# Last products of a graph layer taken by halves of TensorE's rows, and its bias added by transfers, in a planned four-layer kernel

## The chip, the cores and the metric

One NeuronCore of one Trainium2 chip runs the whole program in one launch. The metric is the device time of one execution in microseconds (us). The kernel before took 2096.2 us in the median of three runs (2094.66 to 2099.83). The profile pages and the trace come from one further, profiled execution. The engines are named as in the profile: PE is TensorE's matmul, PEld its weight load, DVE is VectorE, ACT is ScalarE, POOL is GpSimd, SP is SyncE, which here only issues transfers.

## What is computed

Four graph layers follow one another on `x` of 8 batches, 2048 nodes and 64 channels, with one 2048 x 2048 adjacency `adj`. Each ends in a residual add and a layer norm. The first one is the one that the change touches:

```python
# layer 0: w[n,k] and b[n] come from each node's embedding of 16 numbers
w = einsum('nd,dkio->nkio', embedding, weight)       # weight: 16 x 3 x 64 x 64
b = einsum('nd,do->no', embedding, bias)
As = [I, A, 2 A A - I]
x_g = einsum('knm,bmc->bnkc', As, x)
x = layernorm(x + einsum('bnki,nkio->bno', x_g, w) + b)
# layer 1: attention with scores s1[i] + s2[j], leaky relu, mask, softmax, elu
# layer 2: (A + I) (x W^T + b) / row sums
# layer 3: three steps of v = W2 relu(W1 [v, A v] + b1) + b2
```

All of it is in f32. The host only lays data out: `adj` and its transpose, `weight` as 192 rows (k, i) by 1024 columns (d, o).

## The kernel before

**Tiles.** The 8 batches are held as four pairs (`p`), two batches of 64 channels side by side in 128 columns: `SX[p]` is 128 nodes x 16 tiles x 128. Nodes also fall into four chunks (`c`) of 512, four tiles each. A *sweep* (lines 1087 to 1122) multiplies one source, such as `SX[p]`, by all of the adjacency: for each chunk 16 products of 128x128 by 128x512 into one PSUM bank (`acc`, line 1106). The adjacency comes from device memory in tiles of 512 KB for every sweep, by SP's queue, through a ring of six buffers (`fetch`, line 244).

**Layer 0.** For a pair, a sweep gives y1 = A x (`y1_chunk`, line 527), stored both transposed, in device memory (`y1_cols`), and as nodes by channels (`SA`, `SB`). A second sweep gives y2 = A y1 (`y2_evict`). Then `second_pass` (line 584) takes the last products, tile by tile: x, y1 and y2 of 128 nodes, transposed, against the weights for 16 embedding dimensions. To use all of TensorE's 128 rows, x and y1 of one batch are stacked on top of each other, 64 channels each, in `xgT` (`stacks`, line 559): x by four transposes and two half copies, y1 by a transfer. One full product with `w01` (128 rows) covers both terms; y2 needs a product of 64 rows per batch with `wk2`, and the two batches' products of this kind run in the two halves of TensorE's rows. So a half of a tile, one `yp` of two PSUM banks, has two full products and one pair of halves (line 609), and the next half takes them in the opposite order. `add_terms` (line 622) scales each of 16 blocks of 64 columns by the node's embedding number (ACT, line 633; for pair 0 every second half on DVE, line 636), sums them by a tree (line 645), and adds them to `SX[p]` (line 647). `first_norm` (line 654) adds the embedding bias `eb` (line 658) and starts the layer norm. `eb` is made once from 16 products of 16 rows (`embedding_bias`, line 376).

**Layer 1.** `scores` finds row maxima on DVE (line 740). `weights` makes the attention weights: two DVE adds (lines 818 and 831) and two ACT functions (826 and 834) for each of 16 tiles, two halves and four pairs; then products with 64 columns for each batch, the two batches in the two halves of TensorE's columns (line 845).

**Layers 2 and 3** are again sweeps with small products at their ends; layer 3 of the last two pairs is one joint product by quarters (line 1219).

**What sets the order.** Nothing is ordered by the hardware alone. Each step is a Python generator; before each piece of work it yields an engine and what it waits for. `Plan` (lines 38 to 110) keeps a time for every engine, adds a cost by formula for each piece, and always emits the piece that could begin first, with ranks for ties, `SLACK` added to what TensorE waits for, and `BACK`, an offset in us for named steps. Sweeps have the last rank: they fill what is left of TensorE's time. The engines then run their own instructions in exactly this order and wait on semaphores. Row tiles of `adj` are loaded at due times of the plan (line 436), and ACT reduces each to a row sum (line 446), from which DVE makes a reciprocal (line 450). The small weights of layers 2 and 3 are centred on DVE (lines 395 to 408) and multiplied on TensorE (`ps_w`, lines 406 to 420), with a copy by ACT between (line 407). Copies that either ACT or DVE can make all go through line 368. POOL issues the transfers of masks, rows and broadcasts (s1b and mb of 1 MB, line 778; mask rows, lines 727 and 813), `sums_of_a`, which adds blocks of the adjacency in device memory by adding transfers (line 1168), and the stores.

## Time and profile before

| | us |
|---|---|
| three runs, median | 2096.2 (2094.66 to 2099.83) |
| the profiled execution | 2099.04 |
| its span, first to last instruction | 2097.3 |
| start of the first product | 6.5 after the span's start |
| start of the first and the last run of line 845 | 447.1 and 1655.8 |
| VectorE: adds of `eb` (line 658), 16 of 0.684 | 10.9 |
| half copies into `xgT` (line 368): ACT 24 of 0.578, DVE 8 of 0.688 | 13.9 and 5.5 |

How to read the profile: the page gives the busy time of each engine and its share of the span, then the same in 40 slices, in tenths. A view of waits lists who waited for whom: us in total, times, the longest. A timeline lists instructions by start, merged where they are alike: start, us from the first start to the last end, engine, line, what is written from what, TensorE's active rows and columns, shapes, and count. A product in f32 is recorded as two instructions. A matmul's end is modelled and overlaps the start of the next one, so the distance from start to start tells what one costs. Windows give each engine's busy time in a stretch, the granted clock of TensorE (1.00 is full speed), the DMA engines' busy share and GB/s.

### The profile page before, as it was taken

To read this page: it belongs to the slowest core of one execution; us is meant where nothing else is said; L and a number is where in the kernel's file an instruction comes from. 1 tells how busy PE (TensorE), PEld (TensorE's weight loads), DVE (VectorE), ACT (ScalarE), POOL (GpSimd) and SP (SyncE) were. 2 spreads that over 40 slices of the span, in tenths; PEclk is the share of its full clock that TensorE was granted. 3 is DMA by queue.
4 is the path that set the end of the run, shared out by engine and by line. 5 is a ranking of instruction groups with operands and counts; after the bars stand their busy time and mean duration, and the time that the engine had idled before them with its cause. 6 is when DMAs were issued, how large, how long until landed. Compare 5 with 4: busy or idle time off the path is not lost.

```text
span 2097.3 us, 19052 instructions
## 1 busy us (share of the span) xinstructions
PE 2065.0 (98%) x6325; PEld 917.1 (44%) x6325; DVE 1461.5 (70%) x1873; ACT 989.0 (47%) x1797; POOL 257.6 (12%) x406
## 2 busy tenths in 40 slices
PE   8999999999999999999999999998999999999997
PEld 3444444444443444444444444443443455444443
DVE  2216756998799999989987979999979732121224
ACT  0014533378877667666266676723757521000002
POOL 2210101211121111112112111001101000000000
PEclk9999999999999999999999999999999999999999
DMA  9798857865475678779969978779787678777785
GB/s 294 257 331 286 299 185 240 277 191 121 130 231 154 161 242 296 235 228 281 336 196 289 286 251 310 245 263 379 226 273 253 217 256 265 268 263 272 265 281 184
DMA packets 221157, 525.22 MB, mean 250 GB/s; under 512 B 21171, under 2 KB 29491, under 8 KB 216691
## 3 DMA queue, kind: packets, MB, share of 16 engines
q1 hardware_dynamic: 170562, 360.20, 51.0%
q0 software_dynamic: 46272, 161.70, 25.1%
q10 hardware_dynamic: 4224, 2.10, 0.4%
q8 instruction: 50, 0.82, 0.2%
q14 instruction: 49, 0.39, 0.1%
HBM read 492.28 MB, written 63.11 MB: 265 GB/s over the span
## 4 chain that ended last, share of the span: by engine, by line
PE 88%; issue 5%; DVE 4%; DMA 2%; ACT 0%; POOL 0%; POOLq 0%; ACTq 0%; DVEq 0%
PE acc L1106 44%; PE yp L609 15%; PE po L845 11%; PE acc L1219 11%; DVE junk L740 2%; PE ps_u L1041 2%; DMA a<-in_adj_t 2%; PE acc L1095 1%; PE acc L1203 1%; DVE terms L645 1%; PE pf L879 1%; PE ps_emb L991 1%; PE ps_sv L690 1%; PE ps_v L1061 0%; PE ps_xT L680 0%
## 5 line engine op out<-in xcount | busy, mean ns | idle before, releaser
L1106 PE MATMUL acc<-a,SX 128*128 128x512 f32 x1152 | 523.7, 600 | 12.5 <-DMA SX<-in_x 6.5
L1106 PE MATMUL acc<-a,SB 128*128 128x512 f32 x768 | 348.6, 597 | 0.4 <-DMA a<-in_adj_t 0.4
L1106 PEld LDWEIGHTS acc<-a,SX 128*128 128x128 f32 x1152 | 214.5, 192 | 276.9 <-issue 259.2
L826 ACT ACTIVATE e<-e,sv 128x1024 f32<-128x1024 f32 x256 | 279.6, 1149 | 80.3 <-DVE e L818 79.5
L633 ACT ACTIVATE terms<-yp,emb_sb 128x128 f32<-128x128 f32 x896 | 243.7, 390 | 130.7 <-PE yp L609 111.9
L831 DVE TENSOR_TENSOR e<-e,mb 128x2048 f32<-128x2048 f32 x128 | 290.4, 2286 | 19.9 <-ACT e L826 19.2
L818 DVE TENSOR_TENSOR e<-s1b,mk 128x2048 f32<-128x2048 f32 x128 | 289.5, 2285 | 8.6 <-PE po L845 7.9
L740 DVE CUSTOM_DVE_ANT_0 junk<-s2b,mr 128x2048 bf16<-128x2048 f32 x128 | 293.0, 2289 | 2.7
L834 ACT ACTIVATE e<-e 128x2048 f32<-128x2048 f32 x128 | 245.0, 1918 | 76.7 <-DVE e L831 76.4
L609 PE MATMUL yp<-SH,xgT 128*128 128x512 f32 x512 | 244.2, 606 | 0.0
L845 PE MATMUL po<-e,SX 128*64 128x512 f32 x1024 | 233.6, 598 | 0.0
L1106 PEld LDWEIGHTS acc<-a,SB 128*128 128x128 f32 x768 | 142.1, 191 | 170.3 <-issue 168.4
L609 PEld LDWEIGHTS yp<-SH,xgT 128*128 128x128 f32 x512 | 90.9, 189 | 137.3 <-issue 131.1
L645 DVE TENSOR_TENSOR terms<-terms 128x512 f32<-128x512 f32 (+1 forms) x176 | 130.0, 739 | 18.5 <-ACT terms L633 14.1
L813 POOL DMA_DIRECT2D mk<-by_col x128 | 71.1, 567 | 518.9 <-DVE e L818 418.3
L845 PEld LDWEIGHTS po<-e,SX 128*64 128x64 f32 x1024 | 67.9, 136 | 147.8 <-issue 135.8
L609 PE MATMUL yp<-SH,y2T 64*128 64x512 f32 x512 | 129.9, 619 | 0.8 <-DVE SB L368 0.8
L1106 PE MATMUL acc<-a,SA 128*128 128x512 f32 x256 | 117.6, 594 | 1.6 <-DMA a<-in_adj_t 1.6
L1219 PE MATMUL acc<-a,t 128*128 128x512 f32 x192 | 85.4, 592 | 0.0
L609 PEld LDWEIGHTS yp<-SH,y2T 64*128 64x128 f32 x512 | 43.2, 185 | 79.6 <-issue 73.7
L636 DVE SCALAR_TENSOR_TENSOR terms<-yp,emb_sb,terms 128x128 f32<-128x128 f32 x128 | 34.6, 344 | 54.8 <-PE yp L609 41.4
L1106 PEld LDWEIGHTS acc<-a,SA 128*128 128x128 f32 x256 | 47.1, 190 | 58.2 <-issue 54.3
(236 smaller groups left out, 1727.0 us busy)
## 6 DMA issues: line engine op xcount, KB each, us to landing
a<-in_adj_t SPq DMA_DIRECT2D x520, 512.0 KB, 5.4
mr<-by_row POOLq DMA_DIRECT2D x64, 512.0 KB, 6.4
mk<-by_col POOLq DMA_DIRECT2D x128, 256.0 KB, 5.6
an<-in_adj SPq DMA_DIRECT2D x16, 1024.0 KB, 11.3
a<-a_plus_i SPq DMA_DIRECT2D x32, 512.0 KB, 5.1
a<-sb SPq DMA_DIRECT2D x24, 512.0 KB, 4.4
a<-sc SPq DMA_DIRECT2D x24, 512.0 KB, 4.3
a<-sd SPq DMA_DIRECT2D x24, 512.0 KB, 4.5
```

The costliest lines, as they stand in the source:

```text
L609: nc.tensor.matmul(yp[:, e, :], lhsT=y2T[rows, cs] if k2 else xg[:, e, cs], rhs=(wk2 if k2 else w01)[rows, hs], start=(k2 == h), stop=(k2 ...
L633: nc.scalar.activation(batches(terms[0][:, dd, :]), term, AF.Copy, scale=weight)
L645: nc.vector.tensor_tensor(a, a, b, ALU.add)
L740: nc.vector.tensor_tensor_reduce(out=junk, in0=s2b[e][0], in1=masks[t][0], scale=1.0, scalar=LOWEST, op0=ALU.add, op1=ALU.max, accum_out=m ...
L813: nc.gpsimd.dma_start(mk, by_col[jt // 2][:, jt % 2, h * HALF : (h + 1) * HALF])
L818: nc.vector.tensor_tensor(e, s1b[0], mk.unsqueeze(1).to_broadcast([P, 2, HALF]), ALU.add)
L826: nc.scalar.activation(e[:, i, :], e[:, i, :], AF.Prelu, bias=sv[:, 2 + i, jt : jt + 1], alpha=ALPHA)
L831: nc.vector.tensor_tensor(e, e, mb[0], ALU.add)
L834: nc.scalar.activation(e, e, AF.Exp)
L845: nc.tensor.matmul(po[i * C : (i + 1) * C, f, :], lhsT=SX[p][:, t, i * C : (i + 1) * C], rhs=e[:, i, f * CW : (f + 1) * CW], start=(t == 0 ...
L1106: nc.tensor.matmul(pa, lhsT=source[:, m, :], rhs=t[:, i, :], start=(m == 0 and not seed), stop=(m == NT - 1),)
L1219: nc.tensor.matmul(pa, lhsT=B[:, 2 * r + b, :], rhs=at_[:, b, :], start=(start and r == 0 and b == 0), stop=(r == RQ - 1 and b == 1), skip ...
```

## The change

Three things change, and with them the order that the plan gives.

- The stacks go. x of both batches is copied whole into `xg[:, 0]` (128 rows: 64 channels of each batch), and y1 comes in the same layout into `xg[:, 1]`. Each term k has its own weights, `wk0`, `wk1`, `wk2`, held twice, in rows 0 to 63 and 64 to 127. Every last product is one of 64 rows, and the two batches' products stand next to each other in the two halves of TensorE's rows: three pairs for half a tile.
- The embedding bias is no longer kept on the chip. It is stored once to device memory, twice side by side for the two batches, and `add_eb` adds it to `SX[p]` chunk by chunk with an adding transfer on POOL's queue, after the first sweep over the pair and the chunk's transposes, and before the last products. DVE's add in `first_norm` goes.
- The plan knows three forms of TensorE's work, full, rows and columns; a piece whose form differs from the one before costs `SWITCH` = 0.2 more. `SLACK` is 0.7 instead of 0.0, `BACK` has six other entries, row tiles are due at 130 + 8.5 t instead of 120 + 9 t, and some waits in layers 2 and 3 also name the earlier stores.

```diff
-    SLACK = 0.0
+    SLACK = 0.7
+    FORMS = ("PE", "PE rows", "PE columns")
+    SWITCH = 0.2
+    HOLD = 0.0
     BACK = {
-        ("add_terms", 0): -3.02,
-        ("finish", None): -0.48,
-        ("scores", 2): -0.01,
+        ("add_terms", 1): -0.79,
+        ("finish", None): -0.22,
+        ("greatest", None): -2.15,
+        ("mask_of_tile", None): -2.68,
+        ("start_chunk", None): -0.33,
+        ("sums", None): 5.39,
     }
@@ def run(self, eng, cost, *after):
+        if eng in self.FORMS:
+            if eng != self.form:
+                cost += self.SWITCH
+            self.form, eng = eng, "PE"
@@ def begins(self, thread):
-        if engs == "PE":
-            ready += self.SLACK
+        if engs in self.FORMS:
+            hold = self.HOLD if engs not in (self.form, "PE") else 0.0
+            return (max(self.free["PE"], ready + self.SLACK + hold), 0, engs)
@@ def constants():
-        nc.sync.dma_start(w01, w0[0:P, :])
...
-        for h in halves:
-            nc.sync.dma_start(wk2[h, :], w0[P : P + C, :])
+        for k, w in enumerate((wk0, wk1, wk2)):
+            for h in halves:
+                nc.sync.dma_start(w[h, :], w0[k * C : (k + 1) * C, :])
...
-        nc.vector.tensor_tensor(w01[0:C, :], w01[0:C, :], wk2[0:C, :], ALU.subtract)
+        nc.vector.tensor_tensor(wk0, wk0, wk2, ALU.subtract)
@@ def embedding_bias():
-        copy(eng, eb, pe)
-        pp_ring.give(k, plan.run(eng, cost(eng, 1024), done))
+        copy(eng, sb, pe)
+        done = plan.run(eng, cost(eng, 1024), done)
+        pp_ring.give(k, done)
+        for e in range(2):
+            nc.gpsimd.dma_start(eb[:, :, e, :], sb)
+            done = plan.dma("DMA", 512, done)
+        at["eb"] = done
@@ def rows_of_adj():
-            yield "SP", [120.0 + 9.0 * t, bc_ring]
+            yield "SP", [130.0 + 8.5 * t, bc_ring]
@@ def stacks():
-            nc.gpsimd.dma_start(
-                xg[C:P], y1_cols[p].rearrange("(e c) n -> c e n", c=C)[:, :, cols(c)]
-            )
+            nc.gpsimd.dma_start(xg[:, 1, :], y1_cols[p][:, cols(c)])
...
-            for e in range(2):
-                eng = yield EITHER, [t_pe]
-                copy(eng, xg[0:C, e, :], pt[e * C : (e + 1) * C])
-                done = plan.run(eng, cost(eng, CW), t_pe)
+            plan.start(1, add_eb(p, c, t_pe))
+            eng = yield EITHER, [t_pe]
+            copy(eng, xg[:, 0, :], pt)
+            done = plan.run(eng, cost(eng, CW), t_pe)
+    def add_eb(p, c, done):
+        yield "DMA", [done, ("y1T", p, NCH - 1), "eb"]
+        nc.gpsimd.dma_start(
+            SX[p][:, tiles(c), :],
+            eb[:, tiles(c), :, :].rearrange("p t e c -> p t (e c)"),
+            accum_op=ALU.add,
+        )
+        at["eb", p, c] = plan.dma("DMA", 450, done, ("y1T", p, NCH - 1), "eb") + 0.5
@@ def second_pass():
-            yield "PE", [("y2", n + 1), ("xg", n + 1)]
+            yield "PE rows", [("y2", n + 1), ("xg", n + 1), ("eb", n // NCH, n % NCH)]
...
-                    for k2 in (h, 1 - h):
+                    for k3, (v, w) in enumerate(((xg[:, 0], wk0), (xg[:, 1], wk1), (y2T, wk2))):
                         for e in range(2):
-                            rows = slice(e * C, (e + 1) * C) if k2 else slice(0, P)
+                            rows = slice(e * C, (e + 1) * C)
                             nc.tensor.matmul(
                                 yp[:, e, :],
-                                lhsT=y2T[rows, cs] if k2 else xg[:, e, cs],
-                                rhs=(wk2 if k2 else w01)[rows, hs],
-                                start=(k2 == h),
-                                stop=(k2 != h),
+                                lhsT=v[rows, cs],
+                                rhs=w[rows, hs],
+                                start=(k3 == 0),
+                                stop=(k3 == 2),
                             )
-                    t_pe = plan.run("PE", 2.8, got)
+                    t_pe = plan.run("PE rows", mm(CW, 3), got)
@@ def first_norm(p, c, done):
-        yield "DVE", [done]
-        v = SX[p][:, tiles(c), :]
-        v4 = v.rearrange("p t (e c) -> p t e c", c=C)
-        nc.vector.tensor_tensor(
-            v4, v4, eb[:, tiles(c), :].unsqueeze(2).to_broadcast([P, TPC, 2, C]), ALU.add
-        )
-        done = plan.run("DVE", dve(CW), done)
-        done = yield from layer_norm(v, CW, done)
+        done = yield from layer_norm(SX[p][:, tiles(c), :], CW, done)
@@ def weights(p, h, jt, s1b, mb, sv, po, ready):
-        done = plan.run("PE", mm(CW, 4) + 0.25, done)
+        done = plan.run("PE columns", mm(CW, 4), done)
@@ def layer2_tail(p, c, z, kz, done):
-        yield "DVE", [done]
+        yield "DVE", [done, *([("stored", 1, c)] if p == NPAIR - 1 else [])]
@@ def u_chunk(p, c, w, dst, bias, s, done):
-        room = {0: ["y1 used"], 1: ["w0 used"]}.get(s, []) if p == 0 else []
+        room = {(0, 0): ["y1 used"], (0, 1): ["w0 used"], (2, 0): [("stored", 0, c)]}.get((p, s), [])
```

More of the change, by code (lines that the diff above doesn't have):

```diff
@@ L59, in __init__ @@
         self.threads = []
+        self.form = "PE"
         self.count = itertools.count()
@@ L269, in resnorm_d4_kernel @@
         fetch(n)
-    w01 = SH[:, 0:8, :].rearrange("p a b -> p (a b)")
+    wk0 = SH[:, 0:8, :].rearrange("p a b -> p (a b)")
     wk2 = SH[:, 8:16, :].rearrange("p a b -> p (a b)")
@@ L342, in resnorm_d4_kernel @@
     rdeg = const.tile([P, NT], F32, name="rdeg")
-    eb = const.tile([P, NT, C], F32, name="eb")
+    wk1 = const.tile([P, D0 * C], F32, name="wk1")
     gv = const.tile([P, P], F32, name="gv")
@@ L359, in resnorm_d4_kernel @@
     }
+    eb = dram.tile([P, NT, 2, C], F32, name="eb")
     y1_cols = [dram.tile([P, N], F32, name=f"y1_cols{p}") for p in range(NPAIR)]
@@ L383, in embedding_bias @@
         done = plan.run("PE", mm(C, NT))
-        eng = yield EITHER, [done]
-        copy(eng, eb, pe)
-        pp_ring.give(k, plan.run(eng, cost(eng, 1024), done))
-        e_ring.give(embT_k, plan.free["PE"])
+        eng = yield EITHER, [done, e_ring]
+        sb, ke = e_ring.take([P, NT, C], "eb_sb")
+        copy(eng, sb, pe)
+        done = plan.run(eng, cost(eng, 1024), done)
+        pp_ring.give(k, done)
+        e_ring.give(embT_k, plan.free["PE"])
+        for e in range(2):
+            nc.gpsimd.dma_start(eb[:, :, e, :], sb)
+            done = plan.dma("DMA", 512, done)
+        e_ring.give(ke, done)
+        at["eb"] = done
     def weights_of_l23():
@@ L439, in rows_of_adj @@
             nc.sync.dma_start(an, adj[t * P : (t + 1) * P, :])
-            done = plan.dma("SP", 1024, bc_ring.t, 120.0 + 9.0 * t)
+            done = plan.dma("SP", 1024, bc_ring.t, 130.0 + 8.5 * t)
             plan.start(1, row_tile(t, an, k, done))
@@ L600, in second_pass @@
                     if h == 0 or ring.ready() > plan.free["PE"]:
-                        yield "PE", [("xg", n + 1), got, ring, *([e_ring] if h == 0 else [])]
+                        yield "PE rows", [("xg", n + 1), got, ring, *([e_ring] if h == 0 else [])]
                     if h == 0:
@@ L839, in weights @@
             return
-        yield "PE", [("made", p, h, jt - 1), done, *([("weighed", p, h, jt - 2)] if jt > 1 else [])]
+        yield "PE columns", [("made", p, h, jt - 1), done, *([("weighed", p, h, jt - 2)] if jt > 1 else [])]
         mine = [held.pop((p, h, t)) for t in (jt - 1, jt)]
@@ L1078, in store @@
         yield from layer_norm(v, CW, done, True)
+        at["stored", p, c] = 0.0
         nc.gpsimd.dma_start(
```

## The prediction

> **What bounds the kernel now.** I read the page first: the busy shares, then the busy tenths by slice.

> ```profile
> PE 2065.0 (98%) x6325; PEld 917.1 (44%) x6325; DVE 1461.5 (70%) x1873; ACT 989.0 (47%) x1797; POOL 257.6 (12%) x406
> ...
> DVE  2216756998799999989987979999979732121224
> ```

> TensorE is busy nearly throughout. VectorE, with 70% overall, is close to full from slice 9 to slice 27: a second limit just under the first. Next, TensorE's own waits:

> ```profile
> PE acc L1106 <- DMA a<-in_adj_t: 8.0, 6, 2.4
> PE acc L1106 <- DMA SX<-in_x: 6.5, 1, 6.5
> PE ps_w L417 <- ACT w32d L407: 3.9, 1, 3.9
> ```

> Outside the start (6.5 us) there are only some 15 us of named waits. So a gain can come from three places: a shorter TensorE program, these waits, or a cost hidden inside "busy". The timeline of TensorE shows such a cost:

> ```profile
> 319.39 1.88 PE L1106 MATMUL acc<-a,SX 128*128 128x512 f32 x4
> 321.11 1.88 PE L609 MATMUL yp<-SH,xgT 128*128 128x512 f32 x4
> 322.92 1.99 PE L609 MATMUL yp<-SH,y2T 64*128 64x512 f32 x8
> 324.83 1.99 PE L609 MATMUL yp<-SH,xgT 128*128 128x512 f32 x4
> 326.65 0.60 PE L539 MATMUL ps_y<-ident,y1T 128*128 128x128 f32 x4
> ```

> The columns are start, duration, and instructions; an f32 product is two instructions. Two full products take 1.72 us from start to start (319.39 to 321.11). The y2T line is four products of 64 rows, each pair running side by side, so it too should take 1.72. But from 321.11 to 326.65 there are 5.54 us for three such units, where 3 x 1.72 is 5.16. The 0.38 is paid at two changes of form, into the halves and out of them: **0.19 to 0.20 us a change**. Around a run of L845 (128*64, halves of columns) the excess is of the same size: 468.06 to 471.65 is 3.59 us for 3.44 of work, with about 0.1 more on each side.

> Last, the two largest stalls, by windows (PE, PEld, DVE, ACT, POOL busy, then the granted clock, DMA share and GB/s):

> ```profile
> 290.00:294.20 4.20, 0.36 (x1) 0.00 (x0) 4.06 (x12) 3.32 (x5) 1.83 (x2) 0.80 0.50 154
> 294.20:299.00 4.80, 4.79 (x12) 3.22 (x13) 3.55 (x8) 0.76 (x4) 1.12 (x2) 0.50 0.77 306
> 1441.00:1453.00 12.00, 5.99 (x14) 2.06 (x13) 11.28 (x8) 4.38 (x4) 1.62 (x3) 1.00 1.04 395
> ```

> At 290 TensorE waits 3.9 us for an ACT copy and then runs 4.8 us at half clock: 3.9 + 2.4 = 6.3 us lost. At 1441 the DMA engines are full (share 1.04), and TensorE loses 6.5 us waiting for tiles of adjacency.

> **The change, part by part.** The profiled execution took 2099.04 us (span 2097.3), 2.8 above the median of the runs, 2096.2. I sum against 2099.0 and take 2.8 off at the end.

> *Products by halves.* For each half of a tile the old code has two full products (1.72) and one pair of halves (0.86); the new one has three pairs (3 x 0.86). That is 2.58 against 2.58, over 128 units: nothing. The saving can only be changes of form. I counted them in the order of instructions that the two programs are built to: 73 into and 73 out of rows, 63 and 63 for columns, 2 for the embedding bias, 274 in all before. After there are 58 + 52 (rows, from and to the full form), 53 + 59 (columns), 12 directly between rows and columns, and 2: 236. 38 fewer x 0.20 = **-7.6 us**, on the engine that sets the end. Most tiles still stand alone between sweep products, so they keep two changes each. The trace has no direct change from rows to columns; between nothing and two ordinary changes its 12 cost 0 to 4.8 us. I take one change each (2.4, in the sum), and keep -10 to -5.

> *The stall at 290.* In the old order ACT's next row reduction (L446) stands ahead of the copy L407. It waits for a reciprocal (L450) that VectorE does only after some 3.5 us of weight centring (L395 to L408); so the copy, and TensorE, wait. In the new order no row reduction stands between that batch and the copy; what TensorE still needs is the last operation of the centring batch (L408's). From the end of the last shared tile, TensorE has about 12.5 us of work up to there, ACT and VectorE about 14.5 (a copy, a reduction, a chunk's norm, 3.4 us of centring). So I expect a wait of about 2 us. Whether the clock falls then decides half of the sum: after 3.9 us it did, after the waits of 2.4 us and less at 1441 it stayed at 1.00. 6.3 - 2 = 4.3; I take **-3.5**, from the ends 0 (the wait returns whole) and -6.3 (it is gone).

> [...]

> *The stall at 1441.* One MB each of s1b and mb, mask rows and the sweep's tiles come together there. The new order has the same loads ahead of the last pair's weighting, beside an equally pure stretch of sweep products. I take **0**, with ends -6.5 (spread out) and +6.5 (pair 2's loads, which now also meet sweep products, stall as well).

> *VectorE and ACT are relieved.* 16 adds of eb go (L658, 0.684 us each: 10.9 us), and 32 half copies of xgT (24 x 0.58 on ACT, 8 x 0.69 on VectorE: 19.4) become 16 whole ones of about 0.6 (10). None is on TensorE's path, so this is worth nothing directly. But the planner uses it: between the first and the last product of L845 the new order has 67 sweep products fewer (782 to 715, 57 us), 10 us less of yp, some 6 of small products, and 32 changes fewer (6.4). That stage lasted 1212 us (447 to 1659), so TensorE would have it done in about 1132. VectorE's work in it is, count by duration, about 1098 us before and 1075 after: 90.6% of the stage becomes 95%. Its idle time halves, from 114 to 57 us. Where VectorE falls behind for a while, TensorE now waits at L845; the weighted products started a median of some 2 us after their exponentials were ready. Setting VectorE's work against TensorE's group by group, the longest stretches in which VectorE falls behind are about 4 us each, two or three of them. I take **+2**; nothing is the lower end, the upper is the third rival's.

> *The bias by transfers.* Two stores of 512 KB and 16 adding transfers of 256 KB. The nearest rows: adding and plain sums L1168 land in 7.9 us in the median, 21.7 at worst; POOL's issues are 0.5 to 1.6 us each, some 18 us on an engine busy for 12%. VectorE's first add into a chunk (L647) now waits for its landing, with everything behind it in VectorE's queue. The cover: the ring of two stacks puts the transfer one whole chunk of products ahead, at least 20 us. **0**; without that cover 16 x 7.9 = 126 us at most. The larger load of w0 (1.5 MB for 1.0) lands long before its use: 0.

> The store of eb goes in runs of 256 B; the nearest row is emb_sb, 128 KB in small runs, 10.5 us to landing, where 256 KB in long runs took 5.0. [...]

> **Sum:** -7.6 - 3.5 + 0 + 2 + 0 = -9.1; 2099.0 - 9.1 = 2089.9, less 2.8: **2087 us**.

> **The rivals.**
> 1. *The order only moves its waits.* The changes of form go (-7.6), but the wait at 290 returns whole and VectorE's lag costs 5: 2096.2 - 7.6 + 5 = 2093.6. For it: every due time is new, and one 4 us wait also halves the clock. Chance 0.27.
> 2. *The transfers spread out as well.* -7.6, both stalls gone (-6.3, -6.5): 2096.2 - 20.4 = 2076. For it: a longer stage of transfers with fewer sweep products beside them; against it: the same bytes, and 5 MB more. Chance 0.13.
> 3. *VectorE becomes the bound* between the first and last L845. If its idle time can't shrink below what it was (114 us: waits for ps_u, pf, the exponentials), the stage lasts 1075 + 114 = 1189, 57 us over TensorE's 1132. It decides from an idle time above 57 us. At 77 it costs 20, net of the same gains 2096.2 - 7.6 - 3.5 + 20 = 2105: slower. For it: 95% leaves little. Against it: stretches of 120 us at 96 to 97% stand in the present trace with TensorE never idle. Chance 0.15.

> **How the numbers follow.** The forecast has 0.45, its own range is 2082 to 2089.9. The measurement tells apart about 0.3%, 6.3 us. The forecast and rival 2 are faster: 0.58; rival 1 is within 0.3%: 0.27; rival 3 slower: 0.15. The range takes in rival 2 with its end (2073) and rival 3 up to 2104, leaving out the dearer half of rival 3 and a little below.

> **What would show it.** Right: the y2T, wk and xgT products of one tile run in steps of 0.43 us without the 0.1 us at their joints; about 236 changes; ps_w's wait near 2 us and no clock of 0.50 after it; the last L845 about 70 to 80 us earlier; TensorE's total wait on ACT and VectorE under 10 us. Wrong: "PE po <- ACT e" among TensorE's longest waits (rival 3); VectorE's add into SX waiting for the eb transfer (the cover); rows and columns changing at more than 0.4 us.

## The result and the profile after

The changed kernel took **2094.69 us** in the median of 12 runs (2090.42 to 2096.64), the kernel before, beside it, 2098.51 (2094.66 to 2101.64, 12 runs). The ratio is 0.998, with a 95% interval of 0.9971 to 0.9989: faster by some 4 us, inside the 0.3% that the prediction called no change. The profiled execution took 2091.89 us (span 2089.8). The forecast was 2087, 9.1 us less than before; measured are 3.8 less. The first rival, an order that only moves its waits, had 2093.6. One run of the experiment e9 below had a lower granted clock (0.85) and took 2403.63 us; its median leaves it out.

The page of the changed kernel, its busy shares and VectorE's tenths (its lines are shifted: 1131 is the sweep's product, 639 the last products, 868 the weighted ones, 469 ACT's row reduction, 384 the copies, 440 `ps_w`):

```profile
PE 2055.0 (98%) x6837; PEld 919.5 (44%) x6837; DVE 1442.0 (69%) x1844; ACT 982.3 (47%) x1794; POOL 267.1 (13%) x424
...
DVE  2317656998899999988999989999796222121224
```

TensorE has 10 us less busy time with 512 instructions more; VectorE's full stretch ends a slice earlier. The view of TensorE's waits (who waited for whom: us in total, times, the longest):

```profile
PE acc L1131 <- DMA a<-in_adj_t: 8.8, 9, 2.3
...
PE yp L639 <- ACT sv L384: 3.4, 1, 3.4
...
PE ps_w L440 <- DVE w32d L431: 0.6, 1, 0.6
```

The wait at `ps_w` is gone but for 0.6 us. In its place stands one that before did not have, `yp` for ACT's copy `sv` (the scores of layer 1, four numbers a node). No line of `po` for ACT's exponentials is there, so rival 3, VectorE as the bound, did not show itself. The timeline of TensorE shows one tile in the new form (start, us, engine, line, what is written from what):

```profile
315.54 1.02 PE L1131 MATMUL acc<-a,SX 128*128 128x512 f32 x2
316.50 1.13 PE L639 MATMUL yp<-SH,xgT 64*128 64x512 f32 x4
317.46 1.02 PE L639 MATMUL yp<-wk,xgT 64*128 64x512 f32 x4
318.32 1.02 PE L639 MATMUL yp<-SH,y2T 64*128 64x512 f32 x4
...
321.85 1.98 PE L1131 MATMUL acc<-a,SB 128*128 128x512 f32 x4
323.67 0.60 PE L562 MATMUL ps_y<-ident,y1T 128*128 128x128 f32 x4
```

Inside the tile every pair stands 0.86 us after the one before, without joints. At each edge 0.96 stands for 0.86, and the product behind the edge takes 0.1 more as well (321.85 to 323.67 is 1.82 for 1.72): two changes a tile, each 0.2, as predicted.

The windows around the new wait (us, then PE, PEld, DVE, ACT, POOL busy, granted clock, DMA share, GB/s), and the timeline of SP's queue and of ACT there:

```profile
246.00:250.00 4.00, 0.57 (x3) 0.30 (x4) 3.90 (x10) 3.60 (x10) 0.54 (x1) 1.00 1.05 397
250.00:254.00 4.00, 4.00 (x12) 1.57 (x10) 3.86 (x12) 2.00 (x2) 0.53 (x1) 0.57 0.97 362
```

```profile
223.98 1.13 SPq L335 DMA_DIRECT2D w2bd<-in_w2t  x2
...
237.60 0.48 SPq L341 DMA_DIRECT2D ivc<-in_iv  x1
238.19 0.82 SPq L462 DMA_DIRECT2D an<-in_adj  x2
```

```profile
243.57 1.91 ACT L469 ACTIVATE an<-an 128x2048 f32<-128x2048 f32 x1 [7.39 <-DMA an<-in_adj]
...
245.48 2.15 ACT L663 ACTIVATE terms<-yp,emb_sb 128x128 f32<-128x128 f32 x8
247.48 1.95 ACT L469 ACTIVATE an<-an 128x2048 f32<-128x2048 f32 x1
...
249.37 0.23 ACT L384 COPY sv<-ps_sv 128x16 f32<-128x16 f32 x1
```

From 224 to 238 us SP issues the 17 small loads of the weights of layers 2 and 3 (the expectations below say 16); the row tile of `adj` stands behind them in its queue. ACT waits 7.4 us for that tile, with the copy `sv` behind the reduction, and TensorE behind the copy, which frees the PSUM buffer that the next `yp` takes. After 3.4 us of waiting the granted clock is 0.57 in the mean of the next 4 us.

**A ledger of TensorE's lost time.** For each two neighbouring products I took the distance from start to start less what the size of the first one needs (0.429 us for 512 columns). What exceeds this by over 0.11 us is counted, half clock included; the price of a change of form is not. In us, by stretch, from the profiled execution of each kernel (a second one of the changed kernel is from the experiment e13, "loads moved" is e1):

| stretch | before | changed | changed, second | changed, loads moved (e1) |
|---|---|---|---|---|
| 0 to 60 | 3.6 | 2.8 | 3.2 | 3.2 |
| 60 to 100 | 2.9 | 0.9 | 0.9 | 0.9 |
| 100 to 160 | 2.4 | 4.5 | 4.9 | 4.6 |
| 160 to 230 | 0.2 | 0.0 | 1.2 | 0.0 |
| 230 to 300 | 6.1 | 5.9 | 8.6 | 0.7 |
| 300 to 1380 | 2.4 | 7.0 | 6.9 | 6.8 |
| 1380 to 1460 | 6.5 | 4.6 | 5.4 | 4.2 |
| 1460 to the end | 1.7 | 2.2 | 2.2 | 1.7 |
| sum | 25.7 | 27.9 | 33.4 | 22.3 |
| start of the last product | 2087.1 | 2080.5 | 2085.8 | 2074.1 |

From before to the changed kernel the last product starts 6.6 us earlier while 2.2 more are lost: TensorE's program itself is 8.8 us shorter. The order of the work took the rest. The 2.0 us between 60 and 100 are no merit of the change: they are a half clock in before's execution, which other executions of one and the same kernel had and had not (last section).

### The profile page after: what moved, and what is told of

It reads as the page before. It is cut to its first block, busy times and chain, and to the rows that moved or that the text cites. A ratio compares the mean times of both kernels' runs of the same rounds, so it can differ in the third digit from the quotient of the medians.

```text
span 2089.8 us, 20094 instructions
## 1 busy us (share of the span) xinstructions
PE 2055.0 (98%) x6837; PEld 919.5 (44%) x6837; DVE 1442.0 (69%) x1844; ACT 982.3 (47%) x1794; POOL 267.1 (13%) x424
## 4 chain that ended last, share of the span: by engine, by line
PE 61%; issue 25%; DVE 9%; DMA 4%; ACT 1%; POOL 0%; SPq 0%; POOLq 0%; DVEq 0%; ACTq 0%
PE acc L1131 35%; PE yp L639 13%; PE po L868 9%; DMA a<-in_adj_t 3%; DVE junk L763 2%; DVE e L841 2%; DVE e L854 2%; DVE terms L675 1%; PE ps_u L1065 1%; PE ps_sv L713 1%; PE acc L1120 1%; PE pf L902 0%; ACT terms L663 0%; PE ps_emb L1014 0%; DMA a_plus_i<-a 0%
## 5 line engine op out<-in xcount | busy, mean ns | idle before, releaser
L1131 PE MATMUL acc<-a,SB 128*128 128x512 f32 x768 | 353.5, 599 | 6.4 <-DMA a<-in_adj_t 5.7
L639 PE MATMUL yp<-SH,xgT 64*128 64x512 f32 x512 | 137.9, 615 | 5.1 <-ACT sv L384 3.4
L639 PE MATMUL yp<-wk,xgT 64*128 64x512 f32 x512 | 132.1, 593 | 0.0
L639 PEld LDWEIGHTS yp<-SH,xgT 64*128 64x128 f32 x512 | 44.3, 186 | 78.1 <-issue 62.9
L522 ACT ACTIVATE ln_sq<-SX 128x512 f32<-128x512 f32 x48 | 30.5, 635 | 101.5 <-DVE SX L1028 43.6
L639 PEld LDWEIGHTS yp<-SH,y2T 64*128 64x128 f32 x512 | 49.9, 188 | 60.8 <-issue 59.9
```

Of the source, the lines that this page charges most:

```text
L639: nc.tensor.matmul(yp[:, e, :], lhsT=v[rows, cs], rhs=w[rows, hs], start=(k3 == 0), stop=(k3 == 2),)
L1131: nc.tensor.matmul(pa, lhsT=source[:, m, :], rhs=t[:, i, :], start=(m == 0 and not seed), stop=(m == NT - 1),)
```

## The experiments

Times are medians beside the kernel before on the same chip, ratios with their 95% interval. All kernels but e2, e3, e4, e5 and e13 start from e1.

**e1: the small loads on another queue.** In the changed kernel, all 17 loads (one line of the edit is shown):

```diff
-                nc.sync.dma_start(t[h, h], src)
+                nc.gpsimd.dma_start(t[h, h], src)
```

> The changed kernel with one edit: the 16 small loads of the weights of layers 2 and 3 go through POOL's queue instead of SP's. The orders of TensorE, VectorE and ACT are the same. Theory A (the new wait of 3.4 us at 246 us comes from these loads: SP issues them from 224 to 238 us, so the row tile behind them is late, ACT waits for it, the copy of sv stands behind it, and the clock then halves): the wait and the half clock go, 3.6 + 1.9 = about 5 us less than the changed kernel, some 2089 to 2090, ratio to the kernel before about 0.996. Rival (the row tile is late because of its buffer or of full DMA engines, not of the queue): the wait stays, 2094 to 2095, ratio 0.998.

Measured 2085.17 (2084.45 to 2089.38), 0.9936 (0.9924 to 0.9948). The row tile is issued 14 us earlier, and ACT has `sv` ready 5.9 us earlier, before TensorE needs it; the timelines of the same two engines, and a window:

```profile
224.46 0.93 SPq L462 DMA_DIRECT2D an<-in_adj  x2
```

```profile
236.46 1.96 ACT L469 ACTIVATE an<-an 128x2048 f32<-128x2048 f32 x1
...
243.51 0.24 ACT L384 COPY sv<-ps_sv 128x16 f32<-128x16 f32 x1
```

```profile
246.00:250.00 4.00, 4.00 (x18) 1.66 (x18) 2.75 (x7) 0.53 (x3) 1.08 (x2) 1.00 0.90 287
```

TensorE is busy at full clock where it stood still: the ledger falls by 5.2 in this stretch. So the cause of the new wait is shown. This version is the fastest of the study.

**e5: the same edit in the kernel before.**

> The kernel before, with the 16 small loads of the weights of layers 2 and 3 issued on POOL's queue and not on SP's; everything else and the order on TensorE, VectorE and ACT stay, 274 changes of form. Theory A: the wait at 290 us in before and the wait at 246 us in the changed kernel are one and the same thing, a copy by ACT behind work that waits for row tiles which stand behind these loads in SP's queue. Then the wait at 290 and its half clock go (about 6 us): 2092 to 2093, and what is left between this kernel and the changed kernel with the same edit (2085.2) is the 38 changes of form alone, 7.6 us. Rival: the wait at 290 comes from VectorE's centring of the weights and the reciprocal behind it, as the prediction had it; then the loads' queue changes nothing: 2098 to 2099, and ps_w keeps its wait of 3.9 us.

Measured 2098.99 (11 runs, 2097.35 to 2100.95), 1.0004 (0.9995 to 1.0012): theory A falls. TensorE's wait there is the same to the tenth:

```profile
PE ps_w L417 <- ACT w32d L407: 3.9, 1, 3.9
```

The waits at 290 before and at 246 after are two different ones. The first is not the loads' queue; what the prediction named, VectorE's centring with a reciprocal behind it and a reduction on ACT behind that, is left standing. The changed order freed TensorE of it, and put a row reduction in front of another copy. Between e5 and e1 lie 13.8 us: in the ledger 4.5 of waits, and 9.2 of program.

**e2: the new plan without the new products.** The kernel before with the plan of the changed one (forms, `SWITCH`, `SLACK`, `BACK`, due times), stacks and the add of `eb` kept; 264 changes of form.

> The kernel before with the changed plan (counted forms, SLACK 0.7, the new BACK, due times and room waits), but with the stacks, the full products and VectorE's add of eb as they were. Its order has 264 changes of form, the kernel before 274, the changed one 236. Theory A (the gain is the changes of form): 10 fewer are worth 2 us, so 2096 to 2098 and a ratio of 0.998 to 1.000, give or take its own waits; about 5.6 us above the changed kernel. Rival (the new plan's settings make the gain, not the halves): 2094 to 2095 like the changed kernel, ratio 0.998 or less.

Measured 2127.58, 1.0138 (1.0123 to 1.0152): outside every expectation. The ledger of this kernel has 54 us of waits, in many places. The plan's new settings gave a poor order with the old products' costs, so this kernel tells nothing about the products.

**e3 and e4: a small product ahead of each half tile**, full (373 changes) or, as a control, in rows (236), in the changed kernel:

```diff
+                    nc.tensor.matmul(yp[:, 0, 0:4], lhsT=ident, rhs=a4, start=True, stop=True)
                     for k3, (v, w) in enumerate(((xg[:, 0], wk0), (xg[:, 1], wk1), (y2T, wk2))):
```

> The changed kernel with one more product of 128 rows by 4 columns ahead of each half tile of layer 0's last products, written over by the products that follow. Not counted in the plan, so the order is the same. It has 373 changes of form, 137 more. Theory A (0.20 us a change): 27 us for the changes and 128 x 0.1 to 0.2 us for the small products themselves, 40 to 50 us above the changed kernel, and 27 us above the next run. Rival (the 0.19 us read off the timeline is an effect of modelled ends and is hidden): the same time as the next run within 5 us.

> The control of the run before it: the same small product, but of 64 rows by 4 columns, in the halves' form; 236 changes, as in the changed kernel. Both theories: 128 x 0.1 to 0.2 us, 13 to 26 us above the changed kernel. The difference to the run before it, divided by 137, is the price of a change: 0.20 us by theory A, near 0 by the rival.

Measured 2128.42, 1.0141 (1.0127 to 1.0154), and 2119.76, 1.0092 (1.0076 to 1.0108). The profiled runs differ by 9.7 us, and the control loses some 6 more in waits: under 16 for 137 changes, 0.11 each and not 0.20. But the control puts its batches' pairs out of step, and a product of four columns is short (0.11 us from start to start in the trace of the changed kernel, line 713, where a weight load there lasts 0.19). By my reading the next weights' load is thus a part of either price, which no run shows alone. I made a cleaner pair.

**e9 and e10: the old form of the products in the new order.** Two full products and one pair of halves for a half tile, as TensorE's old work was, with the plan's costs left as they are, so that every other instruction keeps its place. e9 alternates (261 changes); e10 has `(0, 1)` for `(h, 1 - h)`, so that both halves begin with the full products (373):

```diff
-                    for k3, (v, w) in enumerate(((xg[:, 0], wk0), (xg[:, 1], wk1), (y2T, wk2))):
+                    for k3, k2 in enumerate((h, 1 - h)):
                         for e in range(2):
-                            rows = slice(e * C, (e + 1) * C)
+                            rows = slice(e * C, (e + 1) * C) if k2 else slice(0, P)
...
-                                lhsT=v[rows, cs],
-                                rhs=w[rows, hs],
+                                lhsT=y2T[rows, cs] if k2 else xg[rows, e, cs],
+                                rhs=(wk2 if k2 else (wk0, wk1)[e])[rows, hs],
```

> The changed kernel with the small loads on POOL's queue, in exactly the same order; only the last products of half a tile are two full products and one pair of halves again, in alternating order (full, halves, halves, full), where it had three pairs of halves. The full product of 128 rows mixes the two batches, so the output isn't the reference's; the count and size of TensorE's work is that of the old form. 261 changes of form for 236, 25 more. Theory A (the price is that of changes, 0.20 us each, and two full products cost just what two pairs cost): 5 us more than 2085.2, 2090. Rival 1 (the halves themselves are slower or faster than full products by some per cent): 128 units, 0.05 us each are 6 us on top or below. Rival 2 (changes are covered): 2085.

> As the kernel with alternating order, but both halves of a tile begin with the full products (full, halves, full, halves): the same instructions, counts and order around them, and 373 changes of form for 261 and 236. Theory A: 0.20 us each, 137 more than in the changed kernel with this queue, 27 us: 2112 to 2113; 22 us more than the alternating order. Rival (a change costs 0.1 us or less where a half comes after a full product of the same bank, since part of the cost hides): 2099 or less.

Measured 2091.71 (four runs, 2090.03 to 2093.23; profiled 2090.03), 0.9965 (0.9952 to 0.9978), and **2112.99** (profiled the same), 1.007 (1.0058 to 1.0082), where 2112 to 2113 was expected. The timeline of e10 shows what a tile costs:

```profile
321.21 1.02 PE L639 MATMUL yp<-SH,xgT 128*128 128x512 f32 x2
322.07 1.02 PE L639 MATMUL yp<-wk,xgT 128*128 128x512 f32 x2
323.02 1.13 PE L639 MATMUL yp<-SH,y2T 64*128 64x512 f32 x4
324.08 1.12 PE L639 MATMUL yp<-SH,xgT 128*128 128x512 f32 x2
...
327.05 1.98 PE L1131 MATMUL acc<-a,SB 128*128 128x512 f32 x4
328.87 0.60 PE L562 MATMUL ps_y<-ident,y1T 128*128 128x128 f32 x4
```

From 321.21 to 328.87 are 7.66 us for 6 units of 0.86 and a sweep step of 1.72, 6.88: 0.78 for four changes. The ledgers of e1, e9 and e10 hold 22.3, 21.2 and 22.0, so waits explain nothing. The last product starts 28.2 us later in e10 than in e1, for 137 changes **0.21 each**, and 22.9 later than in e9, for 112 **0.20**. Theory A stands for changes between full and rows, which are nearly all that these edits add. e9 is 5.3 later than e1 with 1.1 less of waits: 6.4 for 25 changes, 1.2 over 25 x 0.208, which would be 0.01 a half tile for the halves' own form.

**e6: fewer changes still.** `HOLD` of the plan 4.0 for 0.0; 197 changes.

> The changed kernel with the small loads on POOL's queue, and HOLD of the plan 4.0 for 0.0: a piece in another form is held back 4 us in the plan, so pieces of one form gather. 197 changes of form in the order that it is built to, for 236: 39 fewer. If a change costs 0.20 and nothing else moves, 7.8 us less than the 2085.2 without the hold: 2077. If the order only moves its waits, waits of 4 to 8 us in other places take the gain: 2081 to 2087. If pieces that are held 4 us keep VectorE or ACT late in layer 1, slower than 2087.

Measured 2133.82, 1.0169 (1.0155 to 1.0183). 39 changes went and 45 us or more came, in the direction of the third expectation and far beyond it. TensorE's waits in this kernel:

```profile
PE po L868 <- ACT e L857: 15.8, 4, 6.8
...
PE yp L639 <- ACT terms L663: 8.7, 5, 4.0
```

As I read it, held pieces come in crowds, and ACT, with VectorE ahead of it, does not deliver for them at once; no run tests that alone. Between 300 and 1380 us the ledger has 56 for e1's 6.8.

**e8: the first two adding transfers later**, held on POOL's queue behind the copy of y2:

> The changed kernel with the small loads on POOL's queue, and the first two adding transfers of the bias held on POOL's queue until y2 of the first chunk has been copied out, some 15 us later; everything else as it is, 236 changes of form. Theory A: the adding transfers at 131 us cause the waits of TensorE for the adjacency at 137 to 143 us (4.6 us, where before had 1.9): the waits fall to about 2, 2082 to 2083. Rival: the waits come from the loads of the sweep and the row tiles themselves: they stay, 2085 within 1.

Measured 2087.81 (2084.38 to 2090.0), 0.9947 (0.9934 to 0.9961). The windows of the changed kernel, where two adding transfers are issued at 131 us, then those of e8:

```profile
137.00:144.00 7.00, 4.27 (x8) 1.45 (x7) 0.00 (x0) 0.00 (x0) 0.00 (x0) 0.79 1.06 312
```

```profile
137.00:144.00 7.00, 6.94 (x17) 2.76 (x15) 0.00 (x0) 0.59 (x1) 0.47 (x1) 1.00 0.88 325
```

The waits did fall there, from 4.6 to 1.9 in the ledger, so the adding transfers cost some 2 to 3 us at that place, half clock included. The other kernels agree: from 100 to 160 us the ledger holds 3.8 to 6.9 in the twelve executions whose adding transfers begin at 130 to 136 us, and 1.5 to 2.4 in those without any (before, e2, e5, e7). But the execution lost 6.8 between 60 and 100 us, ahead of anything that the edit touches, where e1 had 0.9, so that the time can't show the gain.

**e7: no adding transfers.** Plain loads of 128 KB a chunk, and VectorE adds, as before; a new order, 235 changes.

> The changed kernel with the small loads on POOL's queue, but without the adding transfers: the bias is stored once (256 KB... as one copy of 64 channels for a node), and each chunk's 128 KB come back by a plain transfer into a buffer, from which VectorE adds them ahead of the first norm, 16 adds as in before (about 11 us of VectorE). 235 changes of form for 236. Theory A: the adds by VectorE were hidden, and the adding transfers are nearly free too, so the time stays within 3 us of 2085.2, somewhat less (2082 to 2084) since the two adding transfers at 131 us no longer stand beside the sweep's loads, where TensorE loses 4.6 us. Rival: taking 11 us off VectorE matters, since it is at 95% in layer 1: 2088 to 2096.

Measured 2121.34, 1.0111 (1.0097 to 1.0125): 33 to 36 more than e1's two measurements, and neither expectation holds. TensorE's longest waits:

```profile
PE acc L1132 <- DMA a<-in_adj_t: 20.1, 16, 2.4
PE ps_rows L817 <- DVE mx L787: 6.9, 2, 6.5
```

**e15: the same VectorE work in e1's order.** To part VectorE's work from the order, 16 idle operations in the place of the old adds, unknown to the plan:

```diff
+        nc.vector.tensor_tensor(v, v, v, ALU.max)
         done = yield from layer_norm(SX[p][:, tiles(c), :], CW, done)
```

> The changed kernel with the small loads on POOL's queue, in exactly the same order, with 16 more operations of VectorE ahead of the first norm (the maximum of SX with itself, 128x512, which changes nothing), in the place and of the size of the 16 adds of eb that the change took away: 11 us of VectorE back. Theory A (VectorE had cover; the loss of the kernel with plain transfers came from its new order): within 1.5 us of the kernel without them. Rival (VectorE at 95% in layer 1 is a second bound, so relieving it was a part of the gain): 5 to 11 us more.

Measured 2090.28 (2087.51 to 2091.0), 0.9954 (0.9938 to 0.9969), beside 2088.52 for e14, the same kernel without them: 1.8 more, with ranges that overlap. The ledger between 300 and 1380 us has 11.9 for e1's 6.8 and e14's 6.3: in this execution 5 of the 11 us reach TensorE, 1.7 of them as a half clock from 744.8 to 748.2 that the other two did not have. So VectorE's work was covered by half or more; between the two expectations the times do not decide. Of the 33 us and more of e7 its adds explain at most some 5; the rest comes with its new order or its plain loads.

**e11 and e12: what a new order alone costs.** `SWITCH` 0.0 (the plan doesn't count changes), and `SLACK` 0.71 for 0.70.

> The changed kernel with the small loads on POOL's queue, and SWITCH of the plan 0.0 for 0.2: the plan does not count changes of form. It gives another order with 236 changes of form, as many as with counting. Theory A: the counting in the plan does not make the changes fewer, the halves do; this order only has waits in other places, which the other settings were not chosen for: 2090 to 2125. Rival: with 236 changes and no other content changed the time is the same within 4 us: 2082 to 2089.

> The changed kernel with the small loads on POOL's queue, and SLACK 0.71 for 0.70: a change without meaning, after which the plan gives another order from some place on, with 239 changes of form for 236 (0.6 us). Theory A: what the kernels with the hold (2134), the plain transfers (2121) and the old products (2128) lost is the price of any new order under settings that fit one order; then this one loses as well, 5 to 40 us. Rival: it stays within 3 us of 2085.8 (2083 to 2089), and the others lost their time by what they do.

Measured 2098.35 (2094.96 to 2105.78), 0.9998 (0.9988 to 1.0009), and 2091.49 (2089.88 to 2095.85), 0.9966 (0.9954 to 0.9978). Against the two measurements of e1 (2085.2 and, below, 2088.5) a hundredth of a microsecond in a setting cost 3 to 6 us by another order; leaving out the count cost 10 to 13, with the same 236 changes. (e12's three more changes are 0.6 of its loss.) So the count in the plan did not lower the number of changes; the form of the products did. That is what a new order without other content cost, and e6 and e7 stand well above it. For e7 the runs do not tell which of its edits brought the order that waits so long.

**e13 and e14: the changed kernel and e1 once more, on one chip.**

> The changed kernel once more, unaltered, for the spread of its runs with their granted clocks: its profiled run took 2091.9, the median of its runs 2094.7. Theory A: the runs differ in how long TensorE ran at half clock (after the wait at 246 us, and about the small products for the bias at 80 us, where before's profile showed a clock of 0.50 and the changed kernel's 1.00), so the times follow the mean granted clock of each run: 2090 to 2091 at 0.997 to 0.998, 2096 and more at 0.995. Rival: runs of the same clock differ by as much as 4 us, so that the spread comes from waits for transfers.

> The changed kernel with the small loads on POOL's queue once more, beside the changed kernel on the same chip. Theory A: 6 to 9 us less than the changed kernel (2085 to 2086), of which the trace shows 5.6 at the wait at 246 us. Rival: the two differ by no more than 4 us, and the 2085.2 was a good draw.

Measured 2094.42 (2091.77 to 2097.55, 12 runs), 0.9979 (0.9969 to 0.9988), and 2088.52 (2087.43 to 2090.26), 0.9949 (0.9934 to 0.9964): 5.9 between them, where the ledger has 5.2 and, in the second execution, 7.9 for the stretch with the wait. e1's 2085.17, on another chip, is lower than e14 by some 3 us; whether by the chip or by a good draw is open. The second profiled execution of the changed kernel took 2097.2, 5.3 more than the first, and the waits tell the larger part of it:

```profile
PE yp L639 <- ACT sv L384: 7.3, 2, 6.1
```

The same wait was 6.1 us long and not 3.4: the length of a wait for a transfer differs from run to run. The clock alone does not rank the runs: at 0.997 they lie from 2091.8 to 2096.5. So theory A of e13 falls, and the rival stands.

## Why the prediction missed

The sum against the profiled execution was 2089.9; two profiled executions of the changed kernel took 2091.9 and 2097.2, and their middle, 2094.5, is also the median of the runs. So some 4.6 us of the 7.7 are wrong terms, and the rest is the conversion to the median. The conversion moves the forecast time and not the forecast change: of the 9.1 us forecast 7.2 and 1.8 came in the two profiled executions and 3.8 between the medians, so the terms are what failed. Point by point:

- **Changes of form, -7.6: right.** 38 fewer at 0.20 to 0.21 (e9, e10) are 7.6 to 7.9. A change into columns is cheaper, 0.15 (last section), but there are 62 of them for 63, so 37 of the 38 had the full price. TensorE's program became 8.8 to 9.2 shorter in three comparisons (before and changed twice, e5 and e1); the last us or so fits the 0.01 a half tile of e9. A direct change from rows to columns costs what one from full to columns does: 0.53 us from start to start at the joint for 0.52, and 0.48 behind it for both, where 0.43 is the step without a change.
- **The stall at 290, -3.5: the step that failed.** Its own part went further than I said: 6.1 to 0.7 in the ledger, and no half clock. But the sum booked it as a gain of the whole kernel: I looked at what the new order puts ahead of that one copy, and not at what it puts ahead of ACT's other copies. With the 17 small loads ahead of the row tiles in SP's queue, a row reduction now waits 7.4 us and holds `sv`. From 230 to 300 us 0.2 was gained in one execution, and 2.5 lost in the other, where -3.5 stood in the sum. This is the first rival, at another place than the one it named.
- **The stall at 1441, 0:** it shrank from 6.5 to between 4.6 and 5.4, a gain that I did not foresee. So was the 2.0 at 80 us (60 to 100 in the ledger), which was luck. Without these two the miss would be larger.
- **VectorE's lag, +2: too low, and by another mechanism.** Between 300 and 1380 us 4.6 more were lost, about rival 1's 5, in waits of 1.8 and less at `yp`, `ps_rows` and others; `po` never waited for an exponential. The stage of line 868 lasted 1137 us for the 1132 forecast, but it began 13 to 17 us later, so its last product started 57 to 62 us earlier, not 70 to 80. VectorE was busy for 1055 us of it, 93%, not 1075 and 95%. (In the page before, its full stretch reaches slice 31, not 27.) That VectorE's relief is "worth nothing directly" is in doubt: e15 gives 2 us in the medians, within the spread, and 5 in the ledger, for 11.
- **The bias by transfers, 0: too low.** The cover for VectorE held (its adds into `SX`, line 677, waited for no transfer), but the price is paid elsewhere: two adding transfers beside the sweep's loads cost 2 to 3 us at 137 (e8).
- **Less 2.8 for the median: wrong.** It rested on three runs. With 11 to 17 runs before's median is 2098.2 to 2099.2 in every comparison, so its profiled execution was an ordinary run and nothing was to be taken off. That alone is over 2 us.

Rival 2 asked for both stalls to go, and neither wholly did. Rival 3 did not come; e6, where pieces are held back, has the waits of `po` for the exponentials that it named.

## What to carry to other kernels

Where two halves of an array take turns with full products, count the changes of form in the order that is built: each between full and halves of rows costs 0.2 us here, as an edit that adds nothing but changes confirms. When a plan gives a new order, look for what now stands ahead of every short copy on every in-order queue, down to the loads ahead of a load. And before a plan's setting is credited with a gain, try a setting a hundredth away: here that alone moved the time by 3 to 6 us, about as much as the whole change brought.

## What the runs showed of the hardware

- A wait of 2.3 us was followed by half clock. In the changed kernel TensorE waits that long for the adjacency from 137.5 on, and then:

```profile
140.00:141.00 1.00, 1.00 (x3) 0.47 (x3) 0.00 (x0) 0.00 (x0) 0.00 (x0) 1.00 1.00 338
141.00:142.00 1.00, 1.00 (x2) 0.00 (x0) 0.00 (x0) 0.00 (x0) 0.00 (x0) 0.54 1.04 397
142.00:143.00 1.00, 0.59 (x2) 0.29 (x2) 0.00 (x0) 0.00 (x0) 0.00 (x0) 0.50 1.05 406
```

  The clock falls at 141.08, 1.3 us after work has begun again at 139.79. After the waits of 2.4 us and less at 1441 before it had stayed at 1.00, which the prediction set beside its own wait of 2 us. At the same place and with the same order in e5, waits of 2.1 us and less were followed by half clock:

```profile
1442.82:1446.23 3.41, 1.44 (x4) 0.68 (x4) 2.36 (x2) 0.04 (x1) 0.43 (x1) 1.00 1.03 393
1446.23:1453.06 6.83, 5.32 (x7) 1.68 (x6) 6.83 (x5) 4.33 (x4) 1.09 (x2) 0.50 1.04 396
```

```profile
80.00:84.00 4.00, 4.00 (x11) 1.85 (x10) 2.65 (x3) 0.00 (x0) 3.54 (x4) 1.00 0.60 128
```

```profile
80.00:84.00 4.00, 4.00 (x11) 2.33 (x11) 2.49 (x3) 1.01 (x1) 2.23 (x2) 0.50 0.17 42
```

- A change of form is paid in two parts. At the joint 0.52 to 0.53 us stand from start to start for 0.43, whichever of full, rows and columns follow each other. Behind it a step of full or rows takes 0.53, one of columns 0.48: 0.20 us for a change into full or rows, 0.15 into columns.
